# Moving transposes from TensorE to VectorE's 32x32 squares and a trip through DRAM, in a four-layer graph network

## The chip, the cores and the metric

One core of one Trainium2 chip. The metric is the device time of one execution in microseconds (us). The kernel before took 4455.4 us (median of 3 runs, 4454.22 to 4460.22) when the prediction was made. A ratio is the mean time of one kernel's fast runs over the mean of the other's fast runs of the same rounds, so it is not quite the ratio of the medians quoted beside it.

## The reference, cut to what matters

64 batch elements of 256 nodes with 512 features, an adjacency of 256 x 256 zeros and ones each, four layers one after the other, float32:

```python
h = relu(layernorm(x)); x = x + L0(h, adj)   # every layer begins with this norm
h = relu(layernorm(x)); x = x + L1(h, adj)
h = relu(layernorm(x)); x = x + L2(h, adj)
h = relu(layernorm(x)); x = x + L3(h, adj, nodemask)

# L1, 8 heads of 64 (the argument below is mostly here)
dense = leaky_relu(e_self[:, :, :, None] + e_neigh[:, :, None, :], 0.2)
dense = dense + NEG_BIG * (1.0 - A[:, None])
out   = relu(softmax(dense, -1) @ feats + b)
# L2: out = relu(tanh(A * (Xc @ Xp.T)) @ Xp) per head
# L3: agg = adj @ (k * mask);  w = mask * sum(q * agg, -1) / sqrt(512);  softmax(w, nodes) * v
```

## The kernel before

The kernel is written as small tasks per batch element. A planner (in the kernel, before anything runs) simulates engines with the lengths written beside each task, and fixes the order of all instructions; up to five elements are in flight. `BEHIND` says how strongly an earlier element's tasks are preferred.

```python
IN_FLIGHT = 5
BEHIND = 20.0
...
key = (round(start, 2), g.b * BEHIND - task.rest)     # the task with the smallest key is next
...
def turned(c):          # rows of h are turned on TensorE, ScalarE takes them out of PSUM with Relu
    @task(f"ht{layer}{c}", f"hn{layer}" + ..., [("PE", 0.5), ("A", 0.6)], ..., banks=1)
    def _(pt):
        for k in range(KC):
            nc.tensor.transpose(pt[:, k * P:(k + 1) * P], g["hn"][:, c, k * P:(k + 1) * P], ident)
        nc.scalar.activation(g["ht"][:, :, c * P:(c + 1) * P], pt.rearrange("p (k i) -> p k i", k=KC), AF.Relu)
```

Layer 1's chain: the projections on TensorE, two row vectors per head sent through DRAM to all partitions (`en`, `es`), a maximum per row and head on VectorE, a few small operations on VectorE, a small transpose of the maxima on TensorE (`mx`), a second way through DRAM, and then the exponentials. Beside it ScalarE and GpSimd prepare the pairs of heads: GpSimd adds the mask, "the pair add".

```python
nc.vector.tensor_tensor_reduce(junk, g["all:en"][:, h, :], g["neg"][:, c, :], 1.0, -BIG,
                               OP.add, OP.max, st["mx"][:, c, h:h + 1])          # 16 of these per element
...
nc.vector.tensor_tensor(mx, mx, es, OP.add)
nc.vector.tensor_scalar(low, mx, -NEG_BIG / 2, 1e20, op0=OP.add, op1=OP.mult)
nc.vector.scalar_tensor_tensor(low, mx, 0.2, low, op0=OP.mult, op1=OP.min)
nc.vector.tensor_tensor(mx, mx, low, OP.max)
for c in range(NC):
    nc.tensor.transpose(pr[:H, c * P:(c + 1) * P], mx[:, c], ident)
...
nc.gpsimd.tensor_tensor(e, e, g["negt"][:, None].to_broadcast([P, 2, NC, N]), OP.add)   # pair add, 4 per element
```

## Time and profile before

| | before |
|---|---|
| time | 4455.4 us |
| span of the profiled run | 4449.4 us |
| TensorE busy / idle | 4357 / 92 us |
| time between two elements in the steady state | 67.2 us |
| stay of one element in the kernel (issue of its load to issue of its store) | 333 us |

333 / 67.2 is 4.96: the five elements in flight.

A row like that asks a question, and the timeline of the kernel before (start us, length us, then as above) answers it:

```profile
1051.02 0.42 DVE L477 CUSTOM_DVE_ANT_0 junk<-all,neg 128x256 f32<-128x256 f32 x1
...
1051.50 2.39 POOL L513 TENSOR_TENSOR pair<-pair,negt 128x1024 f32<-128x1024 f32 x1 [9.97 <-ACT pair L511]
1051.69 2.22 DVE L488 TENSOR_SCALAR low<-mx 128x16 f32<-128x16 f32 x1
1053.83 0.68 DVE L608 TENSOR_TENSOR pair<-tr,at 128x512 f32<-128x512 f32 x1
```

The small operation starts 0.19 us after GpSimd's pair add and ends with it. The maxima had just finished.

### The profile page before, as it was taken

Reading aid. Unit: us, or ns where it says so; the run is one execution under the profiler, and the core shown is the slowest. Engines: PE = TensorE matmul, PEld = TensorE weight load, DVE = VectorE, ACT = ScalarE, POOL = GpSimd, SP = SyncE. Lnnn points to the kernel's source line nnn. Section 1 sums busy time; section 2 is a strip of 40 time slices with the busy share of each in tenths; the row PEclk is TensorE's granted clock in tenths of the full one; section 3 lists DMA queues with packets and bytes.
Section 4 is the critical chain, followed back from the end, with each engine's and each line's share of the span. In section 5 each row is a group of like instructions: output and inputs, shape, how many; then the busy total and the mean of one; then the engine's idle time right before and its main releaser. Section 6 shows DMA issues by size and latency. Waiting matters only on the chain.

```text
span 4449.4 us, 60495 instructions
## 1 busy us (share of the span) xinstructions
PE 4357.1 (98%) x22850; PEld 2997.4 (67%) x22850; DVE 2761.2 (62%) x7530; ACT 1679.7 (38%) x3333; POOL 1175.1 (26%) x969
## 2 busy tenths in 40 slices
PE   6899999999999999999999999999999999999998
PEld 4666666666666667667666666667667666666665
DVE  4765666666666665666666666666666666666653
ACT  1343333433433443443343333333334334334332
POOL 1321222322322322322322222222223223223220
PEclk9899999999999999999999999999999999999999
DMA  4212112122122121221221221221221221221210
GB/s 127 97 54 79 63 70 86 56 79 84 58 79 78 64 79 69 74 79 67 75 77 69 76 77 65 80 77 61 75 86 60 75 86 60 76 86 57 79 53 15
DMA packets 125382, 323.67 MB, mean 73 GB/s; under 512 B 19040, under 2 KB 66208, under 8 KB 100512
## 3 DMA queue, kind: packets, MB, share of 16 engines
q1 hardware_dynamic: 109568, 311.99, 19.3%
q10 hardware_dynamic: 15520, 7.80, 0.7%
q8 instruction: 179, 2.93, 0.3%
q14 instruction: 115, 0.94, 0.1%
HBM read 284.62 MB, written 35.13 MB: 72 GB/s over the span
## 4 chain that ended last, share of the span: by engine, by line
PE 89%; DVE 2%; DMA 1%; issue 0%; ACT 0%; POOL 0%; SPq 0%; POOLq 0%; DVEq 0%; ACTq 0%
PE tr L296 21%; PE acc L296 19%; PE tr L655 10%; PE acc L538 9%; PE tr L605 6%; PE acc L626 6%; PE tr L365 5%; PE tr L681 5%; PE tr L589 3%; PE tr L639 1%; PE tr L574 1%; PE tr L408 1%; DVE junk L477 1%; PE tr L335 1%; PE tr L301 1%
## 5 line engine op out<-in xcount | busy, mean ns | idle before, releaser
L296 PE MATMUL acc<-wv_s,ht 128*128 128x512 f32 x2048 | 932.0, 598 | 1.9 <-ACT ht L366 1.9
L513 POOL TENSOR_TENSOR pair<-pair,negt 128x1024 f32<-128x1024 f32 x256 | 606.7, 2371 | 801.8 <-ACT pair L511 777.1
L609 ACT ACTIVATE pair<-pair 128x512 f32<-128x512 f32 x512 | 310.0, 627 | 884.7 <-DVE pair L608 878.1
L296 PEld LDWEIGHTS acc<-wv_s,ht 128*128 128x128 f32 x2048 | 379.8, 191 | 379.4 <-issue 366.6
L549 POOL TENSOR_TENSOR xt<-xt,o 128x256 f32<-128x256 f32 x256 | 184.5, 731 | 1546.3 <-DVE o L547 1529.3
L538 PE MATMUL acc<-feats,pair 128*128 128x65 f32 x4096 | 508.4, 276 | 10.2 <-DVE xt L316 5.6
L538 PEld LDWEIGHTS acc<-feats,pair 128*128 128x128 f32 x4096 | 491.6, 195 | 37.6 <-issue 25.9
L511 ACT ACTIVATE pair<-all,ec 128x256 f32<-128x256 f32 x1024 | 453.2, 499 | 85.9 <-PE acc L626 50.4
L296 PE MATMUL tr<-w_s,ht 128*128 128x512 f32 x1024 | 465.7, 598 | 2.9 <-ACT ht L366 2.6
L655 PE MATMUL tr<-ht,m_s 128*128 128x256 f32 x2048 | 457.1, 382 | 0.0
L346 DVE BATCH_NORM_STATS2 stats<-xt 128x6 f32<-128x512 f32 x512 | 340.4, 679 | 141.7 <-DMA xt<-in_x_dram 140.7
L655 PEld LDWEIGHTS tr<-ht,m_s 128*128 128x128 f32 x2048 | 386.1, 191 | 54.5 <-issue 4.2
L366 ACT ACTIVATE ht<-tr 128x512 f32<-128x512 f32 x512 | 279.7, 596 | 357.5 <-PE tr L365 297.3
L477 DVE CUSTOM_DVE_ANT_0 junk<-all,neg 128x256 f32<-128x256 f32 x1024 | 390.0, 445 | 4.7 <-DMA all<-er_d 4.6
L357 DVE TENSOR_SCALAR hn<-xt,mv,rstd 128x512 f32<-128x512 f32 x512 | 267.8, 555 | 185.7 <-POOL rstd L351 169.8
L608 DVE TENSOR_TENSOR pair<-tr,at 128x512 f32<-128x512 f32 x512 | 329.3, 683 | 64.2 <-PE tr L605 60.7
L605 PE MATMUL tr<-xc,xpt 64*128 64x256 f32 x2048 | 333.3, 406 | 0.4 <-DVE pair L608 0.4
L521 ACT ACTIVATE pair<-pair 128x1024 f32<-128x1024 f32 x256 | 269.4, 1058 | 166.6 <-DVE pair L519 158.2
L626 PE MATMUL acc<-pair,xp 128*64 128x256 f32 x2048 | 322.0, 396 | 6.2 <-ACT pair L609 6.1
L296 PEld LDWEIGHTS tr<-w_s,ht 128*128 128x128 f32 x1024 | 190.4, 192 | 193.7 <-issue 185.4
L351 POOL TENSOR_TENSOR rstd<-rstd,power 128x2 f32<-128x2 f32 x256 | 227.7, 890 | 313.2 <-DVE rstd L350 296.4
L519 DVE TENSOR_TENSOR pair<-pair,all 128x1024 f32<-128x1024 f32 x256 | 302.6, 1222 | 9.9 <-POOL pair L513 6.3
(87 smaller groups left out, 5272.9 us busy)
## 6 DMA issues: line engine op xcount, KB each, us to landing
all<-er_d SPq DMA_DIRECT2D x128, 1024.0 KB, 4.5
all<-m_d SPq DMA_DIRECT2D x64, 1024.0 KB, 4.6
xt<-in_x_dram SPq DMA_DIRECT2D x64, 512.0 KB, 3.6
adj<-in_adj_dram SPq DMA_DIRECT2D x128, 256.0 KB, 2.6
out_dram<-xt SPq DMA_DIRECT2D x64, 512.0 KB, 4.8
mask_in<-in_nodemask_dram SPq DMA_DIRECT2D x64, 128.0 KB, 3.2
w_n<-in_L_gnn_Wqk_dram ACTq DMA_DIRECT2D x16, 128.0 KB, 3.8
wv_s<-in_L_gnn_W_v_dram ACTq DMA_DIRECT2D x1, 1024.0 KB
```

The source lines that it names most:

```text
L296: nc.tensor.matmul(p, ht[:, k, c * P:(c + 1) * P], w[:, k], start=(k == 0), stop=(k == KC - 1))
L346: nc.vector.bn_stats(stats[:, c, :], xt[:, c, :])
L477: nc.vector.tensor_tensor_reduce(junk, g["all:en"][:, h, :], g["neg"][:, c, :], 1.0, -BIG, OP.add, OP.max, st["mx"][:, c, h:h + 1])
L511: nc.scalar.activation(e[:, s, j, :], g["all:es"][:, h, :], AF.Prelu, bias=st["ec"][:, j, H + h:H + h + 1], alpha=0.2)
L513: nc.gpsimd.tensor_tensor(e, e, g["negt"][:, None].to_broadcast([P, 2, NC, N]), OP.add)
L519: nc.vector.tensor_tensor(e, e, g["all:m"][:, 2 * p:2 * p + 2, None, :].to_broadcast([P, 2, NC, N]), OP.subtract)
L538: nc.tensor.matmul(po[i][:, h % 4, :], e[:, s, j, i * P:(i + 1) * P], feats[:, j, h, :], start=(j == 0), stop=(j == NC - 1))
L605: nc.tensor.matmul(ps[s][:, m, :], g["xpt"][half, p, m * P:(m + 1) * P], g["xc"][half, p, :], start=True, stop=True)
L608: nc.vector.tensor_tensor(th[:, s], ps[s], g["at"], OP.mult)
L609: nc.scalar.activation(th[:, s], th[:, s], AF.Tanh)
L626: nc.tensor.matmul(pyt[s * U:(s + 1) * U, p % 2, :], g["xp"][:, m, h * U:(h + 1) * U], g[f"pair:th{p}"][:, s, m, :], start=(m == 0), stop= ...
L655: nc.tensor.matmul(pz[:, s, :], m3_s[:, k, d * P:(d + 1) * P], g["ht"][:, k, :], start=(k == 0), stop=(k == KC - 1))
```

## The change

Its intent: TensorE is the bound, so take its transposes away. Rows of every layer, layer 2's projection and its output and the adjacency are transposed in 32x32 squares on VectorE; the squares are written to DRAM and read back in runs of 32 floats, which puts each square in its place. Layer 3 still projects the rows with the combined matrix, but no longer multiplies the projected rows with all rows and masks the products with the adjacency: it sums the neighbours' rows with the adjacency on TensorE and multiplies those sums with the projected rows, row by row, on VectorE. `BEHIND` goes from 20 to 10. The core of the diff (weights in a matching row order, buffers and some pools are cut):

```diff
-BEHIND = 20.0
+BEHIND = 10.0
+    def squares(sq, t):
+        for c in range(NC):
+            nc.vector.transpose(sq.rearrange("p (r k c i) -> p c k r i", r=4, k=KC, c=NC)[:, c], t[:, c])
+        sq_d = rows_d.tile([P, NC * D], F32, name="sq_d")
+        nc.sync.dma_start(sq_d, sq)
+        return sq_d
+    def gathered(t, sq_d):
+        for i in range(4):
+            nc.sync.dma_start(t.rearrange("p k (c b i) -> b p (k c) i", c=NC, b=4)[i],
+                              sq_d.rearrange("(b d) (r f i) -> b (d r) f i", b=4, r=4, i=S)[i])
...
-        @task("at", "load", [("PE", 0.45), ("A", 0.6)], {"at": 1}, {"adj": (1, 2)}, banks=1)
-                    nc.tensor.transpose(pa[:, m, n * P:(n + 1) * P], g["adj"][:, n, m * P:(m + 1) * P], ident)
-            nc.scalar.copy(g["at"], pa)
+                nc.sync.dma_start(g["blocks"][q * S:(q + 1) * S],
+                                  adj[b].rearrange("(a i) (m q j) -> q i m a j", i=S, q=4, j=S)[q])
+        @task("at", "load", [("V", 0.6)], {"at": 1}, {"blocks": 1})
+            nc.vector.transpose(g["at"], g["blocks"].rearrange("p m a j -> p (m a j)"))
...
-            def turned(c):                      # TensorE transposes of the rows, ScalarE's Relu copy
+                shift = ... scalar_tensor_tensor(shift, mean, -1.0, rstd, mult, mult)     # VectorE
+                    nc.scalar.activation(g["hn"][:, c, :], g["xt"][:, c, :], AF.Relu, bias=shift, scale=rstd)
+            @task(f"sq{layer}", f"hn{layer}", [("V", 1.15), ("D", 2.2)], ...)
+            @task(f"ht{layer}", f"sq{layer}", [("D", 2.7)], {"ht": 1})
...
-        def turn_xp(c): ...    def back(c): ...    def times_m(q): ...
+        @task("sqx", "xp0 xp1", [("V", 1.2), ("D", 2.2)], ...)      # squares, then xpt: gathered
+        @task("sqy", "py1 py3", [("V", 1.15), ("D", 2.2)], ...)     # squares, then yr: back as rows
+        def neighbours(c): ...                  # layer 3: sums of neighbours' rows on TensorE
+        def score3(c): ...                      # projected rows times those sums, on VectorE
```

Each element makes six trips through DRAM: rows of four layers, layer 2's projection, layer 2's output.

## The prediction

> **What bounds the kernel now.** I read four views in this order: the page's busy shares, the windows table, the timeline of TensorE over one period, and the DMA issues with the DMA queue's own waits. First the page: its head, its first part, and the chain that ended last.
>
> ```profile
> span 4449.4 us, 60495 instructions
> PE 4357.1 (98%) x22850; PEld 2997.4 (67%) x22850; DVE 2761.2 (62%) x7530; ACT 1679.7 (38%) x3333; POOL 1175.1 (26%) x969
> ...
> PE 89%; DVE 2%; DMA 1%; issue 0%; ACT 0%; POOL 0%; SPq 0%; POOLq 0%; DVEq 0%; ACTq 0%
> ```
>
> TensorE is busy 98% and carries 89% of the chain; no other engine is near it. The windows (us, then PE, PEld, DVE, ACT, POOL busy, granted clock, DMA share) say where the missing 2% lies:
>
> ```profile
> 0.00:50.00 50.00, 13.46 (x42) 7.23 (x43) 26.09 (x67) 0.00 (x0) 5.83 (x16) 1.00 0.84 230
> ...
> 1000.00:2000.00 1000.00, 1000.00 (x5295) 689.74 (x5294) 630.64 (x1745) 389.55 (x775) 273.11 (x223) 1.00 0.21 74
> ...
> 4400.00:4450.00 50.00, 35.89 (x168) 23.36 (x164) 16.34 (x37) 9.88 (x20) 1.97 (x2) 0.90 0.06 22
> ```
>
> In the middle TensorE has no idle time at all. The 92 us of idle time are the start (36.5 us in the first 50, about 20 more up to 300 us) and the end (some 20). So every microsecond taken from TensorE in the steady state is gained, as long as TensorE stays the engine that is always busy.
>
> Now what a piece of TensorE's work costs. [...] the page gives 598 ns for one 512-column matmul, yet eight of them occupy less than 4.8 us. So I take start-to-start differences from the timeline (start us, length us, group):
>
> ```profile
> 1060.94 1.09 PE L365 MATMUL tr<-ident,hn 128*128 128x128 f32 x8
> 1061.88 0.56 PE L538 MATMUL acc<-feats,pair 128*128 128x65 f32 x4
> ...
> 1067.66 3.60 PE L296 MATMUL acc<-wv_s,ht 128*128 128x512 f32 x8
> 1071.10 0.38 PE L492 MATMUL tr<-ident,mx 128*8 128x128 f32 x2
> ...
> 1074.54 7.12 PE L655 MATMUL tr<-ht,m_s 128*128 128x256 f32 x32
> 1081.51 3.60 PE L296 MATMUL acc<-wv_s,ht 128*128 128x512 f32 x8
> 1084.94 3.62 PE L681 MATMUL tr<-ht,cols 128*128 128x256 f32 x16
> 1088.39 3.60 PE L296 MATMUL acc<-wv_s,ht 128*128 128x512 f32 x8
> ```
>
> Four product matmuls of 512 columns (each is two records) take 1071.10 - 1067.66 = 3.44 us; eight transposes 1061.88 - 1060.94 = 0.94 us; the layer 3 projection 6.97 us; the layer 3 scores 3.45 us. One batch element takes 67.2 us: one w1a group starts at 1030.93, its successor at 1098.13.
>
> [...] SyncE waited 74.3 us in 64 waits for its small store of rows (er_d). [...] Here the 16 KB store landed in 1.4 us, which I use for small ones; 512 KB loads and stores are slower:
>
> ```profile
> all<-er_d SPq DMA_DIRECT2D x128, 1024.0 KB, 4.5
> ...
> xt<-in_x_dram SPq DMA_DIRECT2D x64, 512.0 KB, 3.6
> ...
> out_dram<-xt SPq DMA_DIRECT2D x64, 512.0 KB, 4.8
> ```
>
> **The change part by part, per batch element.**
>
> TensorE, removed: 32 transposes of rows; the period holds them as groups of 4, 8, 8 and 12, start to start 0.44 + 0.94 + 0.88 + 1.30 = 3.56 us. The adjacency's four 0.59. Layer 2's two sets of eight 1.02 each. Together 6.2 us. Layer 3 drops the projection (6.97) and the scores (3.45), 10.4 us, and adds four 512-column matmuls for the neighbours' sums (3.44) and eight for the rows times m3 (6.88), 10.3 us. So layer 3's new form is neutral for TensorE: it pays by needing no second adjacency load and by fitting the new layout. Net gain 6.3 us, 64 times 403 us. The floor is 4449 - 403 = 4046 us, a period of 60.9 us.
>
> VectorE now uses 42.4 us of 67.2 (630.64 in 1000). Removed: normalisation 267.8/64 = 4.2, projection copy 0.7, score products 0.96 + 0.17, one of two output adds 0.64. Added: eleven transposes of 512 columns and one of 1024. Estimate [...] as the 512-column SBUF operation of L357 shows with 544 ns: 11 x 0.55 + 1.1 = 7.1. Four small shifts at 0.2 as L350, 0.8. Two score products of 512 columns from PSUM at 0.74 as L316, with their accumulator reads 1.65. Net +2.9, about 45.5 us of 60.9, or 75%. Not the bound on average.
>
> ScalarE loses the four kinds of PSUM copies (279.7 + 36.7 + 68.4 + 37.5 = 422 us) and gains the normalisation (512 x 0.6) and two copies (128 x 0.58), 380 us: neutral. GpSimd: about neutral.
>
> DMA: 10 issues per element become 42. Single packets in the trace took 18 ns (median) at 256 bytes, 46 at 1 KB, 309 at 8 KB, about 9 ns plus 27 bytes a ns. Estimates: a 128-byte packet 13 ns, a 4 KB one 160. Five gathers of 4096 small packets and the adjacency's 2048 are 22,528 x 13 / 16 = 18 us per engine; six stores of 128 x 4 KB 8 us; layer 2's way back 1.5; less 1.3 for the second adjacency load and the mask. With today's 19.3% of 69.5 = 13.4 us this gives about 40 us of 60.9: two thirds busy. SyncE: issues of 320 to 370 ns for simple shapes, some 600 ns for 1024 packets (the weight loads of that count took 588 ns at least), gives about 24 us; six waits for a store to land, 3 us each, 18 us; er and m 3 us. About 45 us of 60.9, in order.
>
> **What this makes of the path.** In the order of the instructions (no time in it) the kernel before repeats after every element; the changed one repeats after five: the five elements in flight run nearly in step through a layer. I added durations from the rows above along one such wave. From layer 1's projections to layer 2's scores VectorE has about 125 us of work and TensorE about 116; in the rest 106 against 188. So for over a third of the wave the engines are level, and each late DMA shows. I take 10 us of new idle time per wave of 5 (estimate; 9 of it is the excess of VectorE), 12.8 waves, 130 us. The start: 35 more weight DMAs on ScalarE at about 0.55 us ahead of its first normalisation, 20 us, with more adjacency loads behind; 25 us. The end: the last elements run their DMA round trips with less beside them, 25 us. Sum: 4046 + 130 + 25 + 25 = 4226, say 4230 us.
>
> **Rivals.**
> (a) TensorE stays full, idle time only at the ends: 4046 + 40, about 4090. For: five elements in flight, and nothing in the steady state waited before. Against: the level stretch and six DMA round trips per element.
> (b) SyncE's in-order queue becomes the bound: each store, wait, and four gathers at 6 to 7 us, five times, plus the rest is 45 us if all sources are ready, but behind a 1 MB broadcast (4.5 us) a store lands later, and a wait for VectorE or a free ht buffer blocks all behind it. If the queue reaches 65 us per element, 64 x 65 + 150 = 4310 to 4400; at 70 us, over 4600. For: SyncE is already shown waiting, but for results (993.6 us for the adjacency's transpose), without harm. Against: 45 is three quarters of 60.9.
> (c) Small packets cost much more than 13 ns (DRAM reads in 128-byte pieces): at twice that, DMA has 58 us of 60.9 and (b) follows.
> (d) VectorE transposes of float32 run at half rate: +7 us per element, 53 us of 60.9, the level stretch grows by some 13 us per wave more: about 4400.
>
> **Range and chances.** (a) is the lower end: 4090. (b) in its mild form and (d) give the upper: 4410. I give (a) 0.15, my sum or near it 0.55, mild (b) or (d) 0.2, bad (b) or (c) 0.1. Two per cent is 89 us; below 4366 counts as faster: 0.77; within 0.14; slower 0.09.
>
> **What would show it.** TensorE busy near 3960 us; transposes of 128x512 near 550 ns; VectorE busy near 2950 us; DMA share near 60%; gathers landing in under 5 us; in the middle windows TensorE at 95 to 98% with idle time released by VectorE in layers 1 and 2. If instead TensorE's idle time is ended by DMA into ht or xpt, and SyncE shows hardly a gap, (b) or (c) holds and the time is above my figure; transposes near 1.1 us mean (d).

## More of the kernel before

The prediction shows the lines that say TensorE bounds the kernel. These are others, groups of VectorE (line, engine, operation, tiles, shapes, count, then busy us and mean ns of one, then the idle time before them and what ended it):

```profile
L477 DVE CUSTOM_DVE_ANT_0 junk<-all,neg 128x256 f32<-128x256 f32 x1024 | 390.0, 445 | 4.7 <-DMA all<-er_d 4.6
L488 DVE TENSOR_SCALAR low<-mx 128x16 f32<-128x16 f32 x64 | 126.5, 1977 | 2.1
L489 DVE SCALAR_TENSOR_TENSOR low<-mx,low 128x16 f32<-128x16 f32 x64 | 12.8, 201 | 0.1
```

The first row is the maxima. The second is an operation of 16 columns that takes 1977 ns, where its neighbour of the same size in the third takes 201.

## The result, and the profile after

5007.38 us median (4992.91 to 5017.83, 4 runs), beside 4454.81 for the kernel before in the same rounds; ratio 1.1238, 95% interval 1.1201 to 1.1274. Slower by 12%, and 780 us above the prediction. The page of the changed kernel: span, busy shares, and the granted clock in tenths, slice by slice (9 stands for 90% or more).

```profile
span 4996.8 us, 55008 instructions
PE 4297.5 (86%) x17986; PEld 2551.3 (51%) x17986; DVE 3212.0 (64%) x7914; ACT 1743.3 (35%) x3205; POOL 1297.2 (26%) x1097
...
PEclk9889889889889889889889889879979979989979
```

The instruction count of TensorE fell as intended (22850 to 17986), but its busy time fell by only 60 us and 607 us of idle time came in. The clock row repeats with a period of three slices: TensorE ran at half clock for part of every wave of five elements. Two windows of one wave (us; then PE, PEld, DVE, ACT, POOL busy, clock, DMA share, GB/s):

```profile
747.00:900.00 153.00, 152.54 (x561) 78.62 (x560) 89.93 (x227) 46.19 (x91) 25.45 (x23) 1.00 0.64 146
900.00:1087.00 187.00, 142.43 (x642) 97.06 (x642) 132.63 (x337) 72.41 (x132) 67.14 (x52) 0.78 0.54 146
```

For 153 us TensorE is full at full clock. In the next 187 us, where the five elements go through layer 1, it is idle for 45 us and has a clock of 0.78.

Busy time at half clock is not the same as work, so I split the span in this way: idle time is the span less the union of all matmul records; "half clock" is half of the busy time that lies in intervals of clock 0.5 (the only other value in these traces is 1.0), that is, an estimate of the time which full clock would have saved (four matmuls of L634 took 1.23 us at clock 0.50 and 0.70 us soon after at 1.0); the rest is work at full speed.

| us | span | work at full speed | half clock | idle |
|---|---|---|---|---|
| before | 4449 | 4331 | 26 | 92 |
| changed | 4997 | 3949 | 348 | 699 |
| difference | +547 | -382 | +322 | +607 |

So the intended gain is there, some 380 us of it, and it is eaten by waits and by the clock. The split is rough: in the runs below the same TensorE instructions come to between 3879 and 4052 us of work at full speed. What TensorE waited for in the changed kernel (us in total, times, longest):

```profile
PE tr L522 <- DVE mx L520: 249.3, 27, 16.5
PE acc L568 <- ACT pair L551: 88.0, 28, 6.4
PE tr L438 <- ACT ex L334: 84.9, 12, 9.2
```

In the kernel before this wait for the maxima was all but absent (1.2 us in 2 waits): from the end of the last operation on `mx` to the transpose of it lay 15.7 us (median) of slack in which TensorE did other work. In the changed kernel the slack is 0.4 us. While TensorE stands at that transpose, ready products behind it in its order do not start: ahead of the transpose at 969.58 us, shown below, the last semaphore that the next product (L309) waited for had come 7.2 us before, and that product started 0.39 us after the transpose. The VectorE groups that answer to those of before:

```profile
L507 DVE CUSTOM_DVE_ANT_0 junk<-all,adj 128x256 f32<-128x256 f32 x1024 | 546.9, 595 | 116.5 <-DMA all<-er_d 116.4
L315 DVE STREAM_TRANSPOSE sq<-hn 128x512 f32<-128x512 f32 x512 | 350.1, 694 | 61.4 <-ACT hn L387 57.8 <-DMA sq_d<-sq 1.3
L315 DVE STREAM_TRANSPOSE sq<-xp 128x512 f32<-128x512 f32 x128 | 141.0, 1102 | 8.9 <-DMA sq_d<-sq 7.1
L385 DVE SCALAR_TENSOR_TENSOR shift<-mv,rstd 128x2 f32<-128x2 f32 x256 | 96.8, 378 | 184.3 <-POOL rstd L379 183.0
L667 DVE STREAM_TRANSPOSE sq<-cols 128x1024 f32<-128x1024 f32 x64 | 78.9, 1232 | 49.0 <-ACT cols L658 49.0
```

The maxima, untouched by the change, went from 445 to 595 ns. A `shift` of two columns takes 378 ns in the mean. The timeline of one of the long waits for them (13.94 us; the longest took 16.5), with all engines in one view:

```profile
962.95 0.42 DVE L507 CUSTOM_DVE_ANT_0 junk<-all,adj 128x256 f32<-128x256 f32 x1
963.17 4.89 POOL L543 TENSOR_TENSOR pair<-pair,negt 128x1024 f32<-128x1024 f32 x2 [6.05 <-ACT pair L541]
...
963.30 2.56 DVE L507 CUSTOM_DVE_ANT_0 junk<-all,adj 128x256 f32<-128x256 f32 x1
...
965.79 2.55 DVE L507 CUSTOM_DVE_ANT_0 junk<-all,adj 128x256 f32<-128x256 f32 x1
...
968.27 0.41 DVE L507 CUSTOM_DVE_ANT_0 junk<-all,adj 128x256 f32<-128x256 f32 x1
...
969.58 0.59 PE L522 MATMUL tr<-ident,mx 128*8 128x128 f32 x2 [13.94 <-DVE mx L520]
```

One maximum takes 0.42 us until GpSimd starts two pair adds; then two maxima take 2.56 and 2.55 us, each ending with one of the pair adds, and the next takes 0.41 again. TensorE stood idle for 13.94 us before it. The two long maxima explain 4.3 us of that; the rest had begun before them, as VectorE could start this element's maxima only at 958.79 us, when the row broadcast from DRAM had landed. I counted this in the trace: maxima clear of any pair add took 418 ns in the mean, those of which half or more lay inside a pair add 2011 ns, 114 of 1024; in the kernel before these are 16 of 1024. The statistics of 512 columns (`stats`), with one input, take 679 ns inside a pair add or outside it, and the transposes of rows 705 or 694.

So some operations of VectorE did not run beside a pair add here: the mean of the maxima went from 418 to 2011 ns, and in the timeline the ends coincide. Below I call this the lock. What the two engines share there, the traces do not show. It also accounts for the odd row of the kernel before: in the timeline shown there the pair add starts less than 0.1 us after the last maximum has ended, and only the 16-column operation waits 2 us, inside the slack. 56 of those 64 operations lie inside a pair add and take 2212 ns; the 7 that are clear of any take 304.

The way through DRAM did not take 4.9 us per trip as the plan has it (2.2 + 2.7). For the rows and the projection, store issue to the first gather's issue took 4.3 us (median), the four gathers' issues 3.7 us, and the last landed about 3 us later: some 11 us, six times per element. In the mean of the run the DMA engines were not full:

```profile
q1 hardware_dynamic: 1641472, 706.39, 57.0%
```

That is an average. Ahead of and during the wait shown above they were (columns as in the two windows above; the last but one is the DMA share):

```profile
950.00:956.00 6.00, 3.48 (x16) 3.29 (x16) 2.81 (x7) 2.11 (x3) 0.72 (x1) 0.70 0.98 254
956.00:964.00 8.00, 0.00 (x0) 0.00 (x0) 5.52 (x28) 2.61 (x7) 1.55 (x2) 0.50 0.91 260
```

Counted in the traces, 31% of all slices of 3 us have a DMA share above 0.9, against 5% in the kernel before. Whether these bursts delay the broadcasts and gathers, and by how much, no run tells apart from the rest of the way.

### The profile page after: what moved, and what is told of

Same layout as the page of the kernel before. It is cut to its first block, busy times and chain, and to the rows that moved or that the text cites. A ratio compares the mean times of both kernels' runs of the same rounds, so it can differ in the third digit from the quotient of the medians.

```text
span 4996.8 us, 55008 instructions
## 1 busy us (share of the span) xinstructions
PE 4297.5 (86%) x17986; PEld 2551.3 (51%) x17986; DVE 3212.0 (64%) x7914; ACT 1743.3 (35%) x3205; POOL 1297.2 (26%) x1097
## 5 line engine op out<-in xcount | busy, mean ns | idle before, releaser
L309 PE MATMUL acc<-wv_s,ht 128*128 128x512 f32 x2048 | 969.8, 618 | 0.0
L568 PE MATMUL acc<-feats,pair 128*128 128x65 f32 x4096 | 606.4, 315 | 88.3 <-ACT pair L551 88.0
L568 PEld LDWEIGHTS acc<-feats,pair 128*128 128x128 f32 x4096 | 590.9, 231 | 156.0 <-ACT pair L551 111.9
L387 ACT ACTIVATE hn<-xt,shift,rstd 128x512 f32<-128x512 f32 x512 | 392.7, 807 | 741.9 <-DVE shift L385 417.0
L507 DVE CUSTOM_DVE_ANT_0 junk<-all,adj 128x256 f32<-128x256 f32 x1024 | 546.9, 595 | 116.5 <-DMA all<-er_d 116.4
L309 PEld LDWEIGHTS acc<-wv_s,ht 128*128 128x128 f32 x2048 | 393.7, 199 | 444.5 <-issue 437.7
L309 PE MATMUL tr<-w_s,ht 128*128 128x512 f32 x1024 | 484.9, 620 | 3.3 <-DMA ht<-sq_d 3.3
L309 PE MATMUL tr<-m_s,ht 128*128 128x512 f32 x1024 | 467.0, 599 | 5.5 <-ACT cols L700 5.5
L634 PE MATMUL tr<-xc,xpt 64*128 64x256 f32 x2048 | 363.1, 440 | 54.7 <-DVE xc L620 22.3
L315 DVE STREAM_TRANSPOSE sq<-hn 128x512 f32<-128x512 f32 x512 | 350.1, 694 | 61.4 <-ACT hn L387 57.8
L549 DVE TENSOR_TENSOR pair<-pair,all 128x1024 f32<-128x1024 f32 x256 | 333.0, 1318 | 54.7 <-POOL pair L543 40.4
L309 PE MATMUL tr<-w1a_s,ht 128*128 128x272 f32 x1024 | 285.2, 435 | 80.6 <-ACT pair L541 45.9
L634 PEld LDWEIGHTS tr<-xc,xpt 64*128 64x128 f32 x2048 | 218.1, 204 | 197.5 <-issue 53.3
```

The source lines that it names most:

```text
L309: nc.tensor.matmul(p, ht[:, k, c * P:(c + 1) * P], w[:, k], start=(k == 0), stop=(k == KC - 1))
L315: nc.vector.transpose(sq.rearrange("p (r k c i) -> p c k r i", r=4, k=KC, c=NC)[:, c], t[:, c])
L387: nc.scalar.activation(g["hn"][:, c, :], g["xt"][:, c, :], AF.Relu, bias=shift[:, c:c + 1], scale=st["rstd"][:, c:c + 1])
L549: nc.vector.tensor_tensor(e, e, g["all:m"][:, 2 * p:2 * p + 2, None, :].to_broadcast([P, 2, NC, N]), OP.subtract)
L568: nc.tensor.matmul(po[i][:, h % 4, :], e[:, s, j, i * P:(i + 1) * P], feats[:, j, h, :], start=(j == 0), stop=(j == NC - 1))
L634: nc.tensor.matmul(ps[s][:, m, :], g["xpt"][half, p, m * P:(m + 1) * P], g["xc"][half, p, :], start=True, stop=True)
```

## The experiments

The first theories were two rivals: (1) the wave order, in which five elements go through layer 1 together, and (2) the length of the way through DRAM. The first seven runs test these. What they left over brought up two more: (3) VectorE's work on layer 1's chain, made longer by the lock with GpSimd, and (4) the half clock, which can be a cost by itself or only a sign of waits. Each of the four can be taken away, but a kernel without (1) or (2) gets a new plan with it; the runs for (3) and (4) keep the order of the run that they change.

A "one-element order" below is one that repeats after every element; the changed kernel's repeats after five. Some runs give a wrong result. "Way removed" means VectorE writes its squares straight into the target tile, in the wrong places.

**The order alone.** The changed kernel with the old weight:

```diff
-BEHIND = 10.0
+BEHIND = 20.0
```

> The changed kernel with one constant put back: BEHIND 20 in place of 10, so that the order repeats after one element, not after five. Theory W (five elements in step make TensorE wait in layer 1, and the waits bring the half clock): TensorE's idle time falls from 700 us to under 250, the mean clock rises from 0.89 to over 0.97, the time to 4100 to 4350 us. Theory D (the way through DRAM itself, its 22,500 small packets and SyncE's queue, delays everything): the order changes little; 4800 to 5100 us, clock under 0.92.

Measured: 5347.8 us, ratio 1.2003, clock 0.865, right result; slower than either theory allowed. The same weight the other way round, in the kernel before:

```diff
-BEHIND = 20.0
+BEHIND = 10.0
```

> The kernel before with one constant changed: BEHIND 10 in place of 20, which makes its order repeat after five elements too. There are no squares and no way through DRAM in it. Theory W: it loses much of what the changed kernel lost, 4700 to 5000 us, with a clock under 0.95 and idle TensorE in layer 1. Theory D: it stays within 2% of 4455 us.

Measured: 4762.3 us, ratio 1.0682 (1.0664 to 1.0700), clock 0.955. The wave order costs the kernel before 307 us, yet without it the changed kernel is slower still, by 340 us. The order matters for hundreds of microseconds and is not by itself the cause: with the trips in, the wave order is the better of the two. That the change lowered `BEHIND` was right for it.

**The way through DRAM.** First only its small packets: four reads of rows of 1 KB in place of the gathers, order untouched. Its output is wrong, which doesn't matter for the time.

```diff
-            nc.sync.dma_start(t.rearrange("p k (c b i) -> b p (k c) i", c=NC, b=4)[i],
-                              sq_d.rearrange("(b d) (r f i) -> b (d r) f i", b=4, r=4, i=S)[i])
+            q = slice(i * NC * D // 4, (i + 1) * NC * D // 4)
+            nc.sync.dma_start(t.rearrange("p k n -> p (k n)")[:, q], sq_d[:, q])
```

> The changed kernel in its own order, but each of the four reads that gather squares takes 1 KB rows as they lie (512 packets in place of 4096); the result is wrong on purpose. Theory W: the DMA share falls to under 45%, the time stays above 4850 us. Theory D: with seven eighths of the small packets gone, most of the loss goes: under 4550 us.

Measured: 4865.2 us, ratio 1.0907; the queue's share fell from 57.0% to 43.9%. Both signs of theory W held, the time by 15 us only; 142 us come from the shape of the reads. Then the way removed altogether, planned anew with weight 10:

```diff
-            nc.vector.transpose(sq.rearrange(...)[:, c], t[:, c])
-        nc.sync.dma_start(sq_d, sq)
-        (gathers)
+            nc.vector.transpose(ht.rearrange(...)[:, c], t[:, c])     # and xpt, hn likewise
```

> The changed kernel, BEHIND 10 as it is, with VectorE writing the squares straight into ht, xpt and hn: the way through DRAM is gone, all the VectorE work stays; wrong result on purpose. The order still repeats after five elements. If the way through DRAM (waits, packets, SyncE's queue) is the main cause: under 4450 us and TensorE idle under 250 us. If the order of five in step with VectorE's added work is the main cause: above 4700 us, about as the kernel before with BEHIND 10 (4762 us) less the transposes.

Measured: 4769.0 us, ratio 1.0708. Still 315 us slower than the kernel before, with no trip at all. And in a one-element order (weight 20):

> As the last, with BEHIND 20: no way through DRAM and an order that repeats after one element. Both suspected causes are away, only VectorE's added work remains: if these two are the causes, TensorE is idle under 150 us and the time is 4050 to 4200 us, clear of the kernel before. If VectorE's added and stretched work is a cause by itself: 4350 us or more.

Measured: 4502.7 us, ratio 1.0109 (1.0088 to 1.0130), work at full speed 3901 us. Here, with trips and waves gone, 386 us of idle and 217 us of half clock are left. Neither the wave order nor the way can be the cause of these, so both first theories leave something over; the waits name the place:

```profile
PE tr L517 <- DVE mx L515: 195.4, 60, 6.2
PE tr L433 <- DVE qk L423: 66.0, 58, 3.8
...
L502 DVE CUSTOM_DVE_ANT_0 junk<-all,adj 128x256 f32<-128x256 f32 x1024 | 661.4, 692 | 4.0 <-DMA all<-er_d 4.0
```

(The first two lines are from the view of waits, the last from the groups of VectorE.) The maxima are at 692 ns, and nearly every element waits for them (60 waits, 64 elements).

**The plan with true lengths.** The changed kernel with the DRAM steps set to measured lengths (5 us for the store, 6 to 6.5 for the gathers, 9.5 to 10 for layer 1's two ways), weight 40 for a one-element order, right result:

```diff
-            @task(f"sq{layer}", f"hn{layer}", [("V", 1.15), ("D", 2.2)], {"sq": 1},
+            @task(f"sq{layer}", f"hn{layer}", [("V", 1.35), ("D", 5.0)], {"sq": 1},
-            @task(f"ht{layer}", f"sq{layer}", [("D", 2.7)], {"ht": 1})
+            @task(f"ht{layer}", f"sq{layer}", [("D", 6.5)], {"ht": 1})
```

> The changed kernel complete and correct; only what the plan assumes is changed: the DMA steps at their measured lengths (store 5, gather 6.5 us from first issue, row broadcasts 10 and 9.5, maxima 2.5), and BEHIND 40, with which the order repeats after one element. If the loss comes from an order laid out on too short waits: idle TensorE under 300 us, 4200 to 4450 us. If the five elements in flight cannot cover the chain however it is ordered: idle and cold time remain, 4700 us or more.

Measured: 5226.0 us, ratio 1.1727. True DRAM lengths do not mend the plan. TensorE's waits moved to layer 3, whose sums waited 416 us for the normed rows.

**The adjacency alone.** In the kernel before, only the adjacency's transposes go to VectorE, right result (the loads and buffers of the edit are cut):

```diff
-BEHIND = 20.0
+BEHIND = 25.0
-        @task("at", "load", [("PE", 0.45), ("A", 0.6)], {"at": 1}, {"adj": (1, 2)}, banks=1)
+        @task("at", "load", [("V", 0.6)], {"at": 1}, {"blocks": 1})
+            nc.vector.transpose(g["at"], g["blocks"].rearrange("p m a j -> p (m a j)"))
```

> The kernel before with one part of the change: the adjacency transposed by squares from a blocked load (no store to DRAM), BEHIND 25, order of one element. It takes 0.6 us of TensorE per element away and puts no round trip on the chain: if the mechanism is right, TensorE stays full and the time falls by 20 to 40 us, to 4415 to 4435 us.

Measured: 4704.9 us, ratio 1.0568. One transposition less on TensorE cost 251 us; TensorE waits 135 us for `hn` in 63 waits. The new order also brought maxima and pair adds together: 121 maxima lie inside one, and their mean went from 445 to 559 ns. To tell the part from the new order that it brings, the same with the planned order of every engine untouched (with one tile for the blocks, so loads run ahead of their use, and the result is wrong, relative error 0.13):

```diff
         @task("at", "load", [("PE", 0.45), ("A", 0.6)], {"at": 1}, {"adj": (1, 2)}, banks=1)
         def _(pa):
-            (four TensorE transposes, ScalarE copy)
+            nc.vector.transpose(g["at"], blocks[0].rearrange("p m a j -> p (m a j)"))
```

> The kernel before with its planned order left untouched in every engine, and only the adjacency transposed by VectorE in 32x32 squares from a second, blocked load: four transposes and one copy per element fall away (4 x 129 ns = 0.5 us of TensorE, 33 us in all), one VectorE operation of 0.6 to 0.7 us comes in, and the result is right. Theory A: the loss in the earlier run of the adjacency alone (4704.9 us) came from its new order, not from the part; then this runs at 4405 to 4440 us. Rival B: the part itself costs (VectorE's operation or the blocked loads stand in the way); then 4500 to 4700 us with new waits.

Measured: 4473.1 us, ratio 1.0042 (1.0029 to 1.0054). Neither expectation: not the gain of 33 us, but 20 us lost in place of 251. So most of the loss in the run before came from the order that the planner made; the part itself is nearly neutral as placed, and with its wrong data this run says no more than that.

**The lock, in the run with trips and waves removed.** One edit in the 4502.7 us run, order untouched: GpSimd's pair add works on 16 of 256 columns (wrong).

```diff
-                nc.gpsimd.tensor_tensor(e, e, g["negt"][:, None].to_broadcast([P, 2, NC, N]), OP.add)
+                nc.gpsimd.tensor_tensor(e[:, :, :, :16], e[:, :, :, :16], g["negt"][:, None, :, :16]..., OP.add)
```

> The run without DRAM step in the one-element order (4502.7 us) with one more edit: GpSimd's pair add (2.35 us, four per element) works on 16 columns of each row of 256 instead of all, so the result is wrong on purpose; nothing else changes. Theory A: GpSimd's long add stretches VectorE's maxima and small operations (mean of the maxima 692 ns against 445 ns in the kernel before), these stand on layer 1's chain, and TensorE waits behind them. Then the maxima go back to 450 to 520 ns, TensorE's idle falls from 386 to below 200 us, and the time is 4150 to 4300 us. Rival B: the remaining loss is the order's distances and not the length of VectorE's work; then the maxima are shorter but the time stays at 4420 to 4500 us.

Measured: 4009.7 us, ratio 0.9003 (0.8989 to 0.9016), clock 0.994. Page, groups and waits:

```profile
PE 3895.7 (97%) x17986; PEld 2302.0 (57%) x17986; DVE 2941.7 (73%) x7914; ACT 1721.2 (43%) x3205; POOL 878.5 (22%) x1097
...
L502 DVE CUSTOM_DVE_ANT_0 junk<-all,adj 128x256 f32<-128x256 f32 x1024 | 404.0, 440 | 5.6 <-DMA all<-er_d 5.6
...
PE tr L517 <- DVE mx L515: 9.2, 2, 4.9
```

VectorE's busy time fell from 3338.6 to 2941.7 us although its instructions are the same; the wait for the maxima fell from 195.4 to 9.2 us; idle is 112 and half clock 16 us. 493 us, more than the expectation allowed. (The cut also shortens the pair's own chain by some 2 us per pair, the mean of the add going from 2407 to 353 ns. That could be a rival for the gain, but in this order nothing waited for it: before the cut the trace shows no wait of TensorE for these exponentials and none of VectorE for the pair add, and VectorE's main wait for GpSimd, that for `rstd`, stays, 128.4 and 129.9 us.)

**The half clock by itself.** In the same 4502.7 us run, three useless products where TensorE waits for the maxima (wrong result, because the way is removed):

```diff
+            for _ in range(3):
+                nc.tensor.matmul(pr, ident, wv3_s[:, 0], start=True, stop=True)
             for c in range(NC):
                 nc.tensor.transpose(pr[:H, c * P:(c + 1) * P], mx[:, c], ident)
```

> The same run without DRAM step (4502.7 us) with three useless 512-column matrix products (3 x 64 x 0.87 us = 166 us of work at the speeds seen) put ahead of the transposes of the layer-1 maxima, where TensorE waits about 3 us per element. Theory A: the half clock that follows such waits costs by itself (217 us in that run), so a TensorE that is kept busy keeps its clock, and the time falls to 4300 to 4420 us with a granted clock above 0.97. Rival B: the half clock is only a sign of waiting and the filler is paid in full where it does not fit a wait; then 4500 to 4670 us.

Measured: 4343.8 us, ratio 0.9754 (0.9740 to 0.9767), clock 0.988. Doing 167 us more work made it 159 us faster: half clock fell from 217 to 42 us and idle from 386 to 232. Before, 6.83 us at half clock had come after a gap of about 3.2 us per element (56 of the 62 half-clock stretches after the start had that length). So the clock is a cost of its own there. In the run with true waits (right result), five such products in the wait of layer 3:

```diff
+                for _ in range(0 if c else 5):
+                    nc.tensor.matmul(pg, ident, wv3_s[:, 0], start=True, stop=True)
```

> The correct run with the plan's steps set to the measured lengths (5226.0 us, idle 743 us, 415 us lost to half clock) with five useless 512-column matrix products ahead of layer 3's neighbour sums, where TensorE waits 6.8 us per element. Theory A (half clock after a wait costs by itself): the wait is filled, the clock stays full for longer, and the time falls by 100 to 300 us to 4930 to 5130 us, with a granted clock of 0.93 or more. Rival B (the filler only takes the place of the wait, and the clock is lost in the other waits anyway): 5200 to 5260 us with the clock near 0.90.

Measured: 5418.8 us, ratio 1.2171, clock 0.881, 193 us slower and outside both expectations. The wait on the normed rows fell from 416 to 158 us, but layer 1's products then waited 214 in place of 129 us for the exponentials, and the half clock rose from 415 to 606 us. Here a filler helped where it closed the main gap of a period (159 us gained), not where others remained (193 us lost).

**The lock in the kernels that keep the DRAM way.** The same cut of the pair add, order untouched, first in the changed kernel itself, then in its one-element order (both wrong):

> The changed kernel itself (5007.4 us), order and DRAM way untouched, with GpSimd's pair add cut to 16 of every 256 columns (wrong on purpose). In the one-element order without DRAM that cut was worth 493 us. Theory A: the stretched VectorE work on layer 1's chain is the main cause here as well; the maxima go from 595 to about 450 ns, VectorE's busy time falls by some 200 us, and the time falls by at least 200 us, to 4550 to 4800 us. Rival B: this order's layer-1 stretch is bound by its distances and by the way through DRAM; VectorE gets shorter, but the time stays above 4900 us.

Measured: 4764.5 us, ratio 1.0705, maxima 424 ns; VectorE's busy time fell from 3212.0 to 2912.3 us. The lock is worth 243 us in the changed kernel, with one reserve: here VectorE had waited 40.4 us for the pair adds themselves, which went with the cut (TensorE's wait for the exponentials stayed, 88.0 and 87.3 us). The larger part of TensorE's wait for the maxima stays without the lock, 164.3 of 249.3 us:

```profile
PE tr L522 <- DVE mx L520: 164.3, 25, 15.3
```

VectorE itself still waits for the row broadcast in front of these maxima, 98.1 us in all.

> The changed kernel with the one-element order (5347.8 us) and the pair add cut to 16 columns (wrong on purpose); the way through DRAM stays whole. Against the run without DRAM step and with the cut (4009.7 us) it prices the way through DRAM alone in an order without the VectorE trouble. Theory A: the way's 845 us in this order came mostly from waits that VectorE's stretched work had set off; then 4050 to 4500 us. Rival B: the trip of some 11 us is too long for this order by itself; then 4800 to 5200 us, with waits of TensorE on the gathered tiles.

Measured: 4886.8 us, ratio 1.0970. Here the lock is worth 461 us, but what stays is far above the 4050 to 4500 of the first theory: the way through DRAM costs 877 us against the 4009.7 us run even where VectorE is not held up. My theory that the trips only cost because of the lock falls.

Together (us, medians):

| | pair add whole | pair add cut, same order | worth of the lock |
|---|---|---|---|
| waves of five, DRAM way (the changed kernel) | 5007 | 4765 | 243 |
| waves of five, way removed | 4769 | not run | |
| one-element order, DRAM way | 5348 | 4887 | 461 |
| one-element order, way removed | 4503 | 4010 | 493 |

The columns compare one order with itself; from row to row the planner makes a new order, so these differences hold the way and the new order together. With that said, one path through the table accounts for the whole distance from 5007 to 4010 us: 238 without the way, 266 more without the waves, 493 more without the lock. Another path gives other shares, as the three act on each other.

**A right result without the lock.** The pair add on VectorE, order untouched, in the changed kernel and in the run with true waits:

```diff
-                nc.gpsimd.tensor_tensor(e, e, g["negt"][:, None].to_broadcast([P, 2, NC, N]), OP.add)
+                nc.vector.tensor_tensor(e, e, g["negt"][:, None].to_broadcast([P, 2, NC, N]), OP.add)
```

> The changed kernel with the pair add on VectorE in place of GpSimd, order untouched; the result is right. VectorE takes four operations of about 1.2 us more per element (307 us in all) and loses the stretching (about 150 ns x 1024 maxima = 154 us and some of the small operations). Theory A: GpSimd's overlap is what hurts, so this is faster than the changed kernel: 4750 to 4950 us, maxima near 450 ns. Rival B: VectorE's length on the layer-1 stretch is what counts, wherever it comes from, and the stretch's 71% of VectorE goes up; then 5000 to 5200 us.

Measured: 4953.6 us, ratio 1.1119, right; 54 us faster than the changed kernel, just short of the first expectation. VectorE is busy for 3216.6 us, where the changed kernel had 3212.0, though it does 324 us more work (256 adds of 1264 ns): so about as much fell away with the lock as the whole add costs.

> The correct run with the plan's steps at the measured lengths (5226.0 us) with the pair add on VectorE, order untouched; the result is right. Theory A: layer 3's sums waited 416 us for the normed rows because VectorE came late; without the overlap it comes earlier and the time falls by 300 us or more, to 4600 to 4900 us. Rival B: the waits are those of the trip through DRAM and stay; then 5150 to 5350 us.

Measured: 4953.7 us, ratio 1.1122, right; 272 us faster than with the add on GpSimd, just short of what the first theory asked. But the wait that should have gone is still there and holds most of the 691 us of idle time:

```profile
PE tr L698 <- ACT hn L387: 475.4, 62, 14.8
```

**More room in the plan, and a sixth element.** In that last run, 12 us (then 4 us) of rest planned ahead of layer 3's sums, right result:

```diff
+        @task("rest3", "hn3", [("D", 12.0)])
-            @task(f"agg{c}", "hn3 am" + ...
+            @task(f"agg{c}", "rest3 am" + ...
```

> The run with true waits and the pair add on VectorE (4953.7 us, correct) with 12 us of rest planned between layer 3's normed rows and the neighbours' sums, where TensorE waited 475 us in all (7.7 us per element); the planner makes a new one-element order, the result stays right. Theory A: the kernel with the DRAM way is held up only by distances that its plan has wrong, and with this one put right TensorE fills; the wait on the normed rows falls below 100 us and the time to 4300 to 4600 us. Rival B: the new order moves the wait elsewhere; TensorE's idle stays above 450 us and the time above 4750 us.

Measured: 4858.5 us, ratio 1.0909, right. The wait moved elsewhere, as the rival said, to layer 1:

```profile
PE acc L568 <- ACT pair L551: 324.0, 121, 5.2
...
PE tr L702 <- ACT hn L387: 21.9, 3, 11.0
```

> The same with 4 us of rest, which gives another one-element order; right result. Theory A: half of the wait goes, 4600 to 4800 us. Rival B: the time depends on the order that comes out rather than on this one distance, and it can fall either side of 4953.7 us with another main wait.

Measured: 5213.8 us, the median of two fast runs (5194.0 and 5233.6; two more, 5302.0 and 5311.5, were slow), ratio 1.1704. 8 us of planned rest less cost 355 us, and the main wait is again the one for the normed rows, 362.6 us: the planner's order, not the one distance, sets the time. Last, a sixth element in flight, in the one-element order with the way and the cut pair add (wrong):

```diff
-IN_FLIGHT = 5 ... X_BUFS = 5 ... AT_BUFS = 5 ... SQUARE_BUFS = 2 ... BLOCK_BUFS = 2
+IN_FLIGHT = 6 ... X_BUFS = 6 ... AT_BUFS = 6 ... SQUARE_BUFS = 1 ... BLOCK_BUFS = 1
```

> The one-element order with the DRAM way and the small pair add (4886.8 us, wrong on purpose) with six elements in flight in place of five: one more input and adjacency buffer each, and one square and one block buffer each in place of two, which pays for them in memory. There an element is in the kernel for 370 us and a new one comes every 74.05 us, so 370 / 74.05 = 5.0 are in flight. Theory A: the way's trips (about 12 us each) lengthen the stay of an element, 298 to 370 us, and with five in flight that sets the period; with six the period falls towards TensorE's own, 65 us or less, and the time to 4150 to 4450 us. Rival B: five in flight is not what holds it, but the order and the other buffers; then the stay grows with the sixth element (over 420 us), and the time stays above 4650 us.

Measured: 4797.4 us, ratio 1.0759. The stay of an element grew from 370 to 434 us and a new one came every 73.2 us in place of 74.05. Six elements in flight only stay longer. So the number in flight is not what holds it, and the first theory falls here too.

What stays open: the 877 us of the DRAM way in the one-element order. It is not the lock (cut there), not the DRAM lengths in the plan as such (true lengths gave 5226 us), not the count in flight. The bursts at full DMA share, named above, are not tested. Each order that I tried waits at another place, and how good an order could be with eleven-microsecond trips in it was not found. No version with a right result beat the kernel before; the best took 4858.5 us.

## Why the prediction was wrong

- **The floor was right.** 403 us of TensorE work were to go; by the split above some 380 went. 4046 us was the floor; 4009.7 us were run when trips, waves and lock were all out of the way (with a wrong result), with TensorE 97% busy. The place was right too: idle time released by VectorE in layers 1 and 2 was a sign named beforehand, and the largest wait is for VectorE's maxima in layer 1.
- **The step that failed** is "I take 10 us of new idle time per wave of 5 (estimate; 9 of it is the excess of VectorE), 12.8 waves, 130 us". In its place stood 607 us of new idle time and 322 us of half clock, 47 and 25 us per wave. (58 of the 607 us lie in the first 300 us, where the prediction had 25 for the start; that leaves 43 per wave.) Three things were wrong in it.
  - It subtracted two sums of busy time, TensorE's 116 us from VectorE's 125, as if the two engines could always be kept full. In the 187 us of the window shown above neither was: TensorE was busy for 142 us and VectorE for 133. TensorE stood at one transpose of the maxima, in the long waits with ready products behind it (ready for 7.2 us in the one shown): 249 us.
  - It took VectorE's durations from the rows of the kernel before, where the order kept maxima and pair adds apart. In the new order they meet: 114 maxima in place of 16 inside a pair add, and the `shift` of two columns took 2300 ns in the 25 cases where it fell inside one. The cut of the pair add in the same order was worth 243 us. The lock was nowhere in the rivals, although the 1977 ns row of 16 columns showed it. But the lock is the smaller part of the wait: with it cut, 164 of the 249 us stay.
  - It gave idle time no price beyond itself. In the traces half clock came with the waits: it cost 348 us in the changed kernel, against 26 in the kernel before, and filling the gaps in one run took it from 217 to 42 us and gave 159 us back.
- **VectorE's transposes** were 694 ns for rows and 1102 for the projection, which reads every fourth column, against an estimate of 550 (from another operation of 512 columns, as the kernel before has no such transpose): with the other sizes and the adjacency 162 us (from (694 - 550) x 512, (1102 - 550) x 128, (698 - 550) x 64 and (1232 - 1100) x 64 ns). VectorE's busy time rose by 451 us, 190 were predicted, so 261 were missed. The lock's stretching was some 300 us in the changed kernel (3212.0 - 2912.3, from the run with the cut pair add in the same order; my count of the operations inside a pair add gives 313, of which 182 are maxima and 54 shifts) and about 146 in the kernel before by the same count, most of it the 16-column operation. So some 154 of the 261 us are the lock; the remaining 107 are these 162 less what other parts took below their estimate. What hurt was not the sum but where the 182 us lie.
- **Rival (c), small packets,** fell as it was stated: a 128-byte packet took 13 ns (median), as estimated, and the queue was busy for 57.0% of 78.1 us per element, 44.5 us, where 40 were predicted. The prediction used this share as an average; the bursts above 0.9 are not in it.
- **Rival (b), SyncE's queue,** was half right: SyncE's issues took 1828 us in all, 28.6 us per element, and a trip took 11 us, but it was never the engine that was always busy. What it lengthened was latency. In the order of five, removing the way gave 238 us.
- **Rival (d), half rate of the transposes,** held for the projection's kind alone (1102 ns, twice the estimate).
- **The order.** That five elements run in step was read off rightly from the order of the instructions, and taken as a cost of 10 us per wave. In the kernel before the same weight costs 307 us.
- **The chances.** The range ended at 4410 us; 5007 us lay outside it, and "slower" had 0.09. Nothing in the rivals added up two waits that feed each other: a late broadcast, then a locked VectorE, then a waiting TensorE at half clock.

## What to carry to other kernels

Work taken off a saturated engine is gained only if the chain around it keeps its slack: look for the longest in-order wait that the new latency can uncover (here the slack fell from 15.7 to 0.4 us), not only for the busy sums of the engines. Look in the profile before for rows whose mean time does not fit their size, 16 columns in 1977 ns: here they showed operations of VectorE that did not run beside one of GpSimd (a maximum took 418 ns clear of a pair add and 2011 inside one), and the new order brought the big ones together. And price a gap on TensorE with the half clock after it: here 322 us of it came in with 607 us of new idle time.

## What the runs show of the hardware

- The half clock: in the run without the way in the one-element order a gap of about 3.2 us (49 of 62 between 3.0 and 3.6) and one of 1.1 us per element were followed by 6.83 us of it nearly every time. In the changed kernel gaps of 1.90 us ahead of 1421.53 us and of 0.24 us ahead of 1422.89 us were followed by 13.6 us at clock 0.50 in which TensorE was busy throughout. The work slowed with the clock: four matmuls of L634 took 1.23 us inside this stretch (at 1432.53) and 0.70 us after it (at 1439.14). The stretch:

```profile
1423.50:1437.10 13.60, 13.60 (x53) 8.05 (x51) 4.90 (x18) 4.69 (x10) 0.62 (x1) 0.50 0.38 117
```

- VectorE's float32 transposes of 32x32 squares: 694 ns for 512 columns, 1102 ns where every fourth column is read, 1232 ns for 1024.
- The lock: 418 ns clear of any pair add and 2011 ns in the mean for maxima that lie at least half inside a pair add of 2.36 us (median), and some 300 us of VectorE time over the changed kernel.
- DMA: a packet took 13 ns for 128 bytes, 18 for 256, 46 for 1 KB (medians), so 0.10, 0.07 and 0.045 ns a byte: a small packet is dear per byte. A whole trip through DRAM with four gathers took about 11 us.
